# Paged attention on one core: moving the loads of the output weights to other slots of the first steps of each half

## Chip, cores and metric

The kernel runs on one core of a Trainium2 chip. The metric is the device time of the whole program in microseconds (us); lower is better.

## What is computed

```python
# x (64, 32, 512); 64 batches of 32 new tokens, 512 hidden, 32 query heads, 8 KV heads, D = 128
x = x + einsum('bct,bcd->bdt', x, W_cond[condition])      # a 32 x 32 matrix for each batch
q, k, v = x @ Wq.T, x @ Wk.T, x @ Wv.T                    # then RMS norm and RoPE on q and k
kc, vc = k_cache[block_table], v_cache[block_table]       # 16 pages of 32 rows: 512 cached keys a batch
scores = q @ concat(kc, k).T / sqrt(D)                    # cached keys masked by the sequence length
o = softmax(scores) @ concat(vc, v)                       # 4 query heads share a KV head
x = x + o.reshape(64, 32, 4096) @ Wo.T                    # output projection
```

All of it is in 32-bit floating point. The output weights Wo are 8 MB.

## The kernel before

**Halves, steps, slots.** The KV heads are taken in two halves (`NHH` = 2) of 4 heads (`GH`), with their 16 query heads each. The 64 batches are taken in 16 tiles (`NT`) of 4 batches (`BT`). A half and a tile make a step: step 0 to 15 are the first half, 16 to 31 the second (`st.n`; `st.t` is the tile, `st.hh` the half). The main loop (L901 to L976) goes through each step in 16 slots; a slot is one batch of the tile and one KV head, `slot = bt * GH + g`. Step 0 begins at slot 4, since its first batch is handled by an opening ahead of the loop.

**What a slot holds.** On TensorE (PE) each slot has the scores of a head (`ps`, L570) and the product with the values of the head before (`po`, L628): about 1.8 us. To this come pieces of the neighbouring steps. At slot 0 stand the scores of the new tokens (`psn`, L588), so that the first `psn` matmul marks the start of a step. At slot 3 stands the K projection of the step ahead (`pp_k`, L401), at slots 4 to 7 the four Q projections of the step ahead (`pp_q`, some 3.6 us each: the long slots), at slot 13 its V projection. At slots 8 and 9 stands the output projection of the step before (`out_proj`, L509 to L526, some 8 us in each of the two slots; slot 8 uses the weights of heads 0 and 1, slot 9 those of heads 2 and 3). At slot 14 the condition matrix is applied to the step after next (`pmix`, L357), and at slot 15 its result is transposed (`px1t`, L365) and copied; in the first half it is also written out for the second half (`x1_b`, L360 to L368: the DMA `x1t_d`, issued by ACT).

**Who orders the work.** The orders of SyncE (SP) and of PE are those in which the code issues (`manual_schedule`, L88); ACT, DVE and POOL are ordered by the scheduler. SP issues nearly all plain loads, in one queue, in this order within a step:

- `load_k` (L277 to L304), at slots 0, 4, 8 and 12, for the batch two ahead: 16 DMAs of 64 KB, one a page (`k_t`; two buffers, so that a load waits until DVE has copied the K of the batch two before it into `kh`, L563).
- `spread` (L460 to L468), at slot 9 (12 DMAs) and slot 11 (4 DMAs): the queries of the step ahead are rearranged, 80 KB each (`q_cols`, and `q_last` for the tile's last batch). The next step's `psn` needs all 16.
- `x1_t` (L341), at slot 13 of the second half: one DMA, read at slot 3 of the next step.
- the weight parts. `load_w` (L234 to L251) loads a quarter of a half's output weights as two parts; a part is 2 DMAs of 256 KB (`wo`, L249). 8 parts, 16 DMAs and 4 MB make up the output weights of a half.

POOL issues the gathers of V (`raw`, L315).

The programs as built show one more order. The DMAs that SP and ACT issue take their completion semaphores from one ring of eight, in turn. An instruction that issues a DMA first waits until the DMA eight places earlier in the ring has landed, whichever of the two engines issued it. Where a DMA of ACT stands in the ring is decided by the scheduler.

**The output weights before.** The rule at L955 asks for part `slot - 10 + st.t * 16` in the first two steps of each half: parts 0 to 5 at slots 10 to 15 of steps 0 and 16, parts 6 and 7 at slots 0 and 1 of steps 1 and 17. They are first read at slot 8 of steps 1 and 17.

Of the kernel before, what the change touches and what calls it, by code (L numbers as in the profile page):

```python
# [27 lines left out]
BT = P // S  # L28
NT = B // BT
NHH = 2  # L30
GH = HK // NHH
# [24 lines left out]
def cond_resid_paged_attention_kernel(  # L56
# [130 lines left out]
    def steps_of(exact, pools):  # L187
# [46 lines left out]
        def load_w(kind, hh, g=0, part=slice(0, 4), eng=nc.sync):  # L234
            if kind == "q":
                src = wq[:, (hh * QH + g * REP) * D : (hh * QH + (g + 1) * REP) * D]
            elif kind == "o":
                src = wo[(hh * QH + g * REP) * D : (hh * QH + (g + 1) * REP) * D, :]
            else:
                src = (wk if kind == "k" else wv)[:, hh * GH * D : (hh + 1) * GH * D]  # L240
            if part.start == 0:
                wt[kind, hh, g] = wpool.tile(
                    [P, 4, 512], F32, tag=f"w{kind}{g}", name=f"w{kind}{g}_{hh}_{uid}"
                )
            t = wt[kind, hh, g]
            if kind == "o" and not exact:
                src = src.rearrange("(h j p) e -> h p j e", h=REP, p=S)
                for h in range(part.start, part.stop):
                    nc.sync.dma_start(t[h * S : (h + 1) * S, :, :], src[h])  # L249
                return  # L250
            eng.dma_start(t[:, part, :], src.rearrange("(c p) e -> p c e", p=P)[:, part, :])  # L251

        def load_parts(which, hh, at):

            if 0 <= at < 2 * len(which):
                load_w(which[at // 2][0], hh, which[at // 2][1], slice(at % 2 * 2, at % 2 * 2 + 2))

        def load_cond_weights(t, eng=nc.sync, kind=mybir.EngineType.SP):
            _, number = nc.values_load_multi_w_load_instructions(
                cond_row[:, t, :],  # L260
                engines=[kind],
                min_val=0,
                max_val=NCOND - 1,
                skip_runtime_bounds_check_because="a batch's condition is one of those there are",
            )
            for i in range(BT):
                blk = slice(i * S, (i + 1) * S)
                eng.dma_start(
                    bd[blk, blk],
                    w_cond.rearrange("(n s) e -> n s e", s=S)[bass.ds(number[i], 1)].rearrange(  # L270
                        "o s e -> (o s) e"
                    ),
                )
# [67 lines left out]
        def x1_a(st):  # L341

            st.acc = work.tile([P, HID], F32, tag="acc", name=f"acc_{st.name}", bufs=3)
            src = acc_d[st.t] if st.hh else x[st.t * P : (st.t + 1) * P, :]
            nc.sync.dma_start(st.acc, src)
# [187 lines left out]
        def new_ot(st):  # L533
            st.ot = act.tile([P, QH, P], F32, tag="ot", name=f"ot_{st.name}", bufs=1)
# [31 lines left out]
        def scores(ba, g):  # L566

            ps = ps_s.tile([P, VC, P], F32, tag="ps", name=f"ps_{ba.name}_{g}")
            for c in range(VC):
                nc.tensor.matmul(  # L570
                    ps[:, c, :],
                    ba.k[g][:, c * P : (c + 1) * P],
                    queries(ba, g),
                    start=True,
                    stop=True,
                )
            pr = work.tile([P, VC, P], F32, tag="pr", name=f"pr_{ba.name}_{g}", bufs=3)
            last["act"] = nc.scalar.activation(pr, ps, AF.Exp, scale=SCALE).ins  # L578
            ba.pr[g] = pr
# [281 lines left out]
        def pieces(st):  # L861
            do = {
                2: (rot_tables,),
                3: (k_a,),
                4: ((q_a, 0),),
                5: ((q_a, 1),),
                6: ((q_a, 2),),
                7: ((q_a, 3),),
                9: ((spread, (0, 1, 3)),),
                11: ((spread, (2,)),),  # L870
                13: (v_a,),
            }
            if st is second:
                do[2] = do[3] = do[13] = ()
            return do
# [22 lines left out]

        x1_a(steps[2])
        load_cond_weights(2)  # L900
        for st in steps:  # L901
            ahead = steps[st.n + 1] if st.n + 1 < len(steps) else None
            beyond = steps[st.n + 2] if st.n + 2 < len(steps) else None
            fill = pieces(ahead) if ahead else {}
            for bt in range(0 if st.n else 1, BT):
                this, after = batch, None
                n = st.n * BT + bt + 2
                if n < NHH * NT * BT:
                    after = Batch(steps[n // BT], n % BT)
                    unfilled += [(after, c) for c in range(VC)]  # L910
                for g in range(GH):
                    slot = bt * GH + g
                    if st.n or slot > GH:
                        scores(this, g)
                    if slot == 0:
                        new_scores(st)
                    if slot in (1, 3):
                        new_values(st, slot - 1)
                    if slot < GH and valued is not None:
                        values(*valued)  # L920
                    for piece in fill.get(slot, ()):
                        if isinstance(piece, tuple):
                            piece[0](ahead, piece[1])
                        else:
                            piece(ahead)
                    if slot in (8, 9) and st.n:
                        out_proj(steps[st.n - 1], slice((slot - 8) * QH // 2, (slot - 7) * QH // 2))
                    if slot == 9:
                        if st.n:
                            new_ot(st)  # L930
                        for ba in turned:
                            turn(ba)
                        turned = []
                        if 0 < st.n < NT // TRIG - 1:
                            tmp = work.tile(
                                [P, 3, TRIG * HD], F32, tag="w1", name=f"trig_{st.n}", bufs=1
                            )
                            with tc.issue_after(last["dve"]), tc.issue_after(last["act"]):
                                angles((st.n + 1) * TRIG, tmp)
                    if slot == 10 and st.n:  # L940
                        store(steps[st.n - 1])
                    if st.n and beyond:
                        if slot == 6 and not beyond.hh:
                            load_cond_weights(beyond.t)
                        if slot == 11:
                            x1_a(beyond)
                    if slot == 13 and beyond:
                        x1_t(beyond)
                    if slot == 14 and beyond:
                        x1_c(beyond)  # L950
                    if slot == 15 and beyond:
                        x1_b(beyond)
                    if slot == 1 and st.n == NT:
                        count(0)
                    if st.t < 2:  # L955
                        load_parts([("o", i) for i in range(GH)], st.hh, slot - 10 + st.t * BT * GH)
                    if st.n in (NT - 2, NT - 1):
                        load_parts(
                            [("k", 0), ("q", 0), ("q", 1), ("q", 2), ("q", 3), ("v", 0)],
                            1,  # L960
                            slot - 5 + (st.n - NT + 2) * BT * GH,
                        )
                    for _ in range({1: 0, GH: 2}.get(slot, 1)):
                        if unfilled and (g or unfilled[0][0] is this):
                            next_values()
                    if slot >= GH and valued is not None:
                        values(*valued)
                    valued = this, g
                    if g == 1 and bt != 1:
                        for ba in turned:  # L970
                            turn(ba)
                        turned = []
                    if later is not None:
                        head_keys(later, g)
                turned.append(this)
                batch, later = later, after  # L976
# [75 lines left out]
```

## Time and profile before

| | us |
|---|---|
| median of three runs | 2204.2 (2204.06 to 2207.32) |
| profiled execution, whole time | 2204.06 |
| its span on the core | 2202.3 |
| first `psn` of steps 0, 1, 2, 3 | 58.27, 103.18, 193.77, 260.90 |
| a regular step of the first half (such as step 2) | 67.13 |
| step 1 | 90.59 |
| first `psn` of steps 16, 17, 18, 19 | 1131.38, 1197.30, 1275.02, 1340.94 |
| a regular step of the second half (such as step 18) | 65.9 |
| step 17 | 77.72 |

The span is the time from the core's first to its last instruction; 1.8 us lie around it. The lengths of the steps are the differences of the starts. A timeline row has the start, the busy time, the engine, the line of the program, the operation with its output and input, and the number of instructions; behind it, in brackets, the idle time before and what ended it. A row of waits has the waiting engine and line, what it waited for, and then the sum in us, the number of times and the longest.

### The profile page before, as it was taken

How to read it: one execution, taken by the hardware profiler on the slowest of the kernel's cores; microseconds unless marked ns; L12 is line 12 of the kernel's file. 1: busy time of each engine (PE TensorE's matmuls, PEld its weight loads, DVE VectorE, ACT ScalarE, POOL GpSimd, SP SyncE). 2: the span in 40 equal slices, each digit the busy share in tenths (PEclk: the TensorE clock that was granted, in tenths of full speed). 3: DMA queues.
4: the chain of work that ended last, by engine and by line, in shares of the span. 5: the costliest groups of instructions: out<-in, count | busy, mean ns of one | idle time of the engine just before them, and what ended most of it. 6: DMA issues, size and time to landing. Idle time of an engine off the chain costs nothing.

```text
span 2202.3 us, 41557 instructions
## 1 busy us (share of the span) xinstructions
PE 2156.6 (98%) x12970; PEld 1502.4 (68%) x12970; DVE 1198.1 (54%) x2881; ACT 867.5 (39%) x1574; POOL 806.1 (37%) x1008
## 2 busy tenths in 40 slices
PE   8889999999999999999999999999999999999998
PEld 5657766677766777666776567776667776667775
DVE  5545466655555654565554555445656445656442
ACT  3424444444333444333433244333334433334441
POOL 4423243333333433333333343334333334334330
PEclk9989999999999999999999999999999999999999
DMA  7575554555555555556766655655555655555551
GB/s 226 160 177 168 159 155 143 165 157 171 155 151 151 158 168 162 154 147 197 238 176 174 165 167 162 176 158 154 148 163 163 174 159 158 149 162 158 174 158 55
DMA packets 387863, 358.77 MB, mean 163 GB/s; under 512 B 54737, under 2 KB 316897, under 8 KB 387633
## 3 DMA queue, kind: packets, MB, share of 16 engines
q1 hardware_dynamic: 342912, 215.10, 34.9%
q0 software_dynamic: 41712, 136.66, 20.9%
q10 hardware_dynamic: 3008, 4.25, 0.5%
q8 instruction: 106, 1.74, 0.3%
q14 instruction: 125, 1.02, 0.2%
HBM read 302.59 MB, written 12.58 MB: 143 GB/s over the span
## 4 chain that ended last, share of the span: by engine, by line
PE 93%; DMA 3%; SPq 2%; issue 1%; ACT 1%; DVE 0%; POOL 0%; DVEq 0%; ACTq 0%; POOLq 0%
PE po_x L628 20%; PE pout_x L516 20%; PE ps_x L570 20%; PE pp_q_x L401 19%; PE pp_k_x L401 5%; PE pp_v_x L401 5%; PE pnv_x L612 2%; PE psn_x L588 1%; SPq L291 1%; DMA k_t_x<-in_kt_dram 1%; PE pmix_x L357 1%; DMA raw_x<-in_vc_dram,v_row 0%; DMA x1t_d<-x1t_x 0%; DMA x1t_x<-x1t_d 0%; DMA wq_x<-in_wq_dram 0%
## 5 line engine op out<-in xcount | busy, mean ns | idle before, releaser
L315 POOL DMA_INDIRECT raw_x<-in_vc_dram,v_row x512 | 538.8, 1052 | 837.9 <-ACT v_x L328 769.3
L578 ACT ACTIVATE pr_x<-ps_x 128x512 f32<-128x512 f32 x512 | 305.8, 597 | 837.4 <-PE ps_x L570 774.4
L628 PEld LDWEIGHTS po_x<-v_x,pr_x 128*128 128x128 f32 x4096 | 516.5, 192 | 125.5 <-issue 114.8
L628 PE MATMUL po_x<-v_x,pr_x 128*128 128x129 f32 x4096 | 551.8, 278 | 0.9 <-ACT v_x L328 0.6
L401 PE MATMUL pp_q_x<-wq_x,x1t_x 128*128 128x512 f32 x1024 | 465.0, 597 | 2.8 <-DMA wq_x<-in_wq_dram 2.8
L516 PE MATMUL pout_x<-wo_x,ot_x 128*128 128x512 f32 x1024 | 451.6, 594 | 0.0
L570 PE MATMUL ps_x<-q_cols_x,kh_x 128*128 128x128 f32 x3072 | 408.7, 276 | 14.2 <-DVE kh_x L563 13.7
L570 PEld LDWEIGHTS ps_x<-q_cols_x,kh_x 128*128 128x128 f32 x3072 | 378.7, 193 | 31.9 <-issue 26.4
L328 ACT ACTIVATE v_x<-raw_x,valid 128x512 f32<-128x512 f32 x512 | 363.0, 716 | 11.6 <-DMA raw_x<-in_vc_dram,v_row 11.2
L516 PEld LDWEIGHTS pout_x<-wo_x,ot_x 128*128 128x128 f32 x1024 | 190.5, 191 | 215.1 <-issue 214.9
L401 PEld LDWEIGHTS pp_q_x<-wq_x,x1t_x 128*128 128x128 f32 x1024 | 186.5, 192 | 189.6 <-issue 186.4
L563 DVE COPY kh_x<-k_t_x 128x512 f32<-128x512 f32 x506 | 205.2, 417 | 181.4 <-PE ps_x L570 151.2
L646 DVE TENSOR_TENSOR nv_x<-po_x,nv_x 128x258 f32<-128x258 f32 x256 | 108.4, 423 | 341.3 <-PE po_x L628 319.9
L418 POOL TENSOR_TENSOR rs_q_x<-ms_q_x,minus_half 128x4 f32<-128x4 f32 x128 | 140.4, 1097 | 176.3 <-DVE ms_q_x L416 176.3
L411 ACT ACTIVATE sq_q_x<-pp_q_x 128x512 f32<-128x512 f32 x128 | 76.6, 598 | 273.6 <-PE pp_q_x L401 186.7
L570 PE MATMUL ps_x<-q_last_x,kh_x 128*128 128x128 f32 x1024 | 135.3, 275 | 0.0
L524 DVE TENSOR_TENSOR acc_x<-pout_x,acc_x 128x512 f32<-128x512 f32 x32 | 22.1, 692 | 200.2 <-PE pout_x L516 200.2
L570 PEld LDWEIGHTS ps_x<-q_last_x,kh_x 128*128 128x128 f32 x1024 | 124.6, 192 | 0.0
L401 PE MATMUL pp_k_x<-wk_x,x1t_x 128*128 128x512 f32 x256 | 117.7, 603 | 3.1 <-DMA x1t_x<-x1t_d 3.0
L415 DVE TENSOR_REDUCE ms_q_x<-sq_q_x 128x4 f32<-128x512 f32 x128 | 86.5, 676 | 54.4 <-ACT sq_q_x L411 52.7
L401 PE MATMUL pp_v_x<-wv_x,x1t_x 128*128 128x512 f32 x256 | 115.2, 592 | 0.0
L649 DVE TENSOR_TENSOR o_x<-nv_x,rden 128x256 f32<-128x256 f32 x256 | 108.5, 424 | 6.5
(105 smaller groups left out, 1464.6 us busy)
## 6 DMA issues: line engine op xcount, KB each, us to landing
k_t_x<-in_kt_dram SPq DMA_DIRECT2D x2048, 64.0 KB
q_cols_x<-rows_x SPq DMA_DIRECT2D x372, 80.0 KB
q_last_x<-rows_x SPq DMA_DIRECT2D x124, 80.0 KB
raw_x<-in_vc_dram,v_row POOLq DMA_INDIRECT x512
wo_x<-in_wo_dram SPq DMA_DIRECT2D x32, 256.0 KB
acc_x<-in_x_dram SPq DMA_DIRECT2D x16, 256.0 KB
x1t_d<-x1t_x ACTq DMA_DIRECT2D x16, 256.0 KB
acc_d<-acc_x SPq DMA_DIRECT2D x16, 256.0 KB
```

The lines of the kernel that those rows point to most:

```text
L315: nc.gpsimd.indirect_dma_start(out=raw.rearrange("p g d -> p (g d)"), out_offset=None, in_=vc, in_offset=bass.IndirectOffsetOnAxis(ap=v_ro ...
L328: nc.scalar.activation(v_bufs[b % 2][:, c, :, 0:D], raw, AF.Copy, scale=ok)
L401: nc.tensor.matmul(pp, st.x1t[:, c, :], w[:, c, :], start=(c == 0), stop=(c == KC - 1))
L415: nc.vector.tensor_reduce(ms, sq, AX.X, ALU.add)
L418: nc.gpsimd.tensor_tensor(rs, ms, minus_half, ALU.pow)
L516: nc.tensor.matmul(st.po, st.ot[:, i, :], wt["o", st.hh, i // 4][:, i % 4, :], start=(i == 0), stop=(i == QH - 1),)
L563: last["dve"] = nc.vector.tensor_copy(k, ba.k_raw[:, :, g, :]).ins
L570: nc.tensor.matmul(ps[:, c, :], ba.k[g][:, c * P : (c + 1) * P], queries(ba, g), start=True, stop=True,)
L578: last["act"] = nc.scalar.activation(pr, ps, AF.Exp, scale=SCALE).ins
L628: nc.tensor.matmul(ba.po[:, g % 2, :], ba.pr[g][:, c, :], ba.v_t[:, c, g, :], start=(c == 0), stop=(c == VC - 1),)
L646: nc.vector.tensor_tensor(t, ba.po, t, ALU.add)
L649: nc.vector.tensor_tensor(ba.o[:, both, :], t[:, :, 0:D], rd.unsqueeze(2).to_broadcast([P, 2, D]), ALU.mult,)
```

## The change

The rule for the output weights is replaced by a table from step and slot to parts.

```diff
+        output_weights = {
+            (0, 4): (0, 1),
+            (0, 5): (2, 3),
+            (0, 6): (4, 5),
+            (1, 4): (6,),
+            (1, 5): (7,),
+            (NT, 10): (0,),
+            (NT + 1, 2): (1,),
+            (NT + 1, 4): (2,),
+            (NT + 1, 5): (3, 4),
+            (NT + 1, 6): (5, 6),
+            (NT + 1, 7): (7,),
+        }
...
-                    if st.t < 2:
-                        load_parts([("o", i) for i in range(GH)], st.hh, slot - 10 + st.t * BT * GH)
+                    for at in output_weights.get((st.n, slot), ()):
+                        load_parts([("o", i) for i in range(GH)], st.hh, at)
```

In the first half parts 0 to 5 (12 DMAs, 3 MB) move from slots 10 to 15 of step 0 to its slots 4 to 6, and parts 6 and 7 from slots 0 and 1 of step 1 to its slots 4 and 5. In the second half part 0 stays at slot 10 of step 16; parts 1 to 5 move from slots 11 to 15 of step 16, and parts 6 and 7 from slots 0 and 1 of step 17, to slots 2 to 7 of step 17. Within a slot the parts stand where they stood: behind the K load, the pieces and `x1_b`.

In the built program the change also moves instructions of engines that the scheduler orders. The place of step 0's last `x1t_d` in the ring of eight goes from between the third and fourth `q_last` DMA of the spread to between the ninth and tenth `wo` DMA. On DVE, the copies `kh` of batch 5 go from behind the norm and rotation of step 1's K to ahead of them, and those of batch 6 and of batch 70 (the third batch of steps 1 and 17) from behind the rotation of the fourth Q projection to between the projections, as they stand in every other step.

## The prediction

> **What bounds the kernel now.** The page's first part says which engine carries the time, its table of waits which waits that engine has.
>
> ```profile
> PE 2156.6 (98%) x12970; PEld 1502.4 (68%) x12970; DVE 1198.1 (54%) x2881; ACT 867.5 (39%) x1574; POOL 806.1 (37%) x1008
> ```
> ```profile
> PE ps_x L570 <- DVE kh_x L563: 13.7, 4, 4.8
> PE psn_x L588 <- DMA q_cols_x<-rows_x: 8.8, 1, 8.8
> ...
> PE pp_k_x L401 <- DMA x1t_x<-x1t_d: 3.0, 1, 3.0
> ```
>
> PE is the bound, and what a load can still give is PE's waits. Where they lie is read from the starts of the steps: all are regular but two. Step 1 takes 90.59 us against 67.13 (23.46 too many), step 17 takes 77.72 against 65.9 (11.8 too many). So the change can gain at most about 35 us, in two places, and I read those two alone. First PE's timeline:
>
> ```profile
> 112.49 0.39 PE L588 MATMUL psn_x<-q_cols_x 128*32 128x128 f32 x1 [8.77 <-DMA q_cols_x<-rows_x]
> ...
> 130.54 1.61 PE L570 MATMUL ps_x<-q_cols_x,kh_x 128*128 128x128 f32 x8 [3.07 <-DVE kh_x L563]
> ...
> 158.20 1.88 PE L570 MATMUL ps_x<-q_cols_x,kh_x 128*128 128x128 f32 x8 [4.83 <-DVE kh_x L563]
> ```
> ```profile
> 1210.08 5.17 PE L401 MATMUL pp_k_x<-wk_x,x1t_x 128*128 128x512 f32 x8 [3.01 <-DMA x1t_x<-x1t_d]
> ...
> 1240.97 2.04 PE L570 MATMUL ps_x<-q_cols_x,kh_x 128*128 128x128 f32 x8 [4.84 <-DVE kh_x L563]
> ```
>
> Step 1 waits 8.77 + 3.07 + 4.83 = 16.7 us; the other 6.8 are matmuls at a low clock after each wait (the scores take 1.6 to 2.0 us there, 1.06 in a regular step). Step 17 waits 7.85 us, and some 4 go the same way. What fed them late stands in SP's timeline:
>
> ```profile
> 93.09 4.85 SPq L465 DMA_DIRECT2D q_cols_x<-rows_x  x8
> 97.99 4.07 SPq L465 DMA_DIRECT2D q_last_x<-rows_x  x4
> 102.10 1.07 SPq L249 DMA_DIRECT2D wo_x<-in_wo_dram  x2
> 103.27 3.07 SPq L465 DMA_DIRECT2D q_cols_x<-rows_x  x4
> 110.61 0.88 SPq L249 DMA_DIRECT2D wo_x<-in_wo_dram  x2
> 112.78 8.75 SPq L291 DMA_DIRECT2D k_t_x<-in_kt_dram  x16
> ```
> ```profile
> 1203.27 3.84 SPq L249 DMA_DIRECT2D wo_x<-in_wo_dram  x6
> 1208.41 15.75 SPq L291 DMA_DIRECT2D k_t_x<-in_kt_dram  x16
> ```
>
> In step 0 the last 4 DMAs of the spread are issued by 106.34 and land 6 us later. SP then stands from 106.34 to 110.61. Its table of waits names the reason, and this is the ring of eight at work: the second part's DMA has to wait for ACT's `x1t_d`, issued at 103.56.
>
> ```profile
> SPq L249 <- DMA x1t_d<-x1t_x: 4.2, 1, 4.2
> ```
>
> How busy the transfers are, the table by windows shows (busy times, then granted clock, DMA share, GB/s):
>
> ```profile
> 60.00:90.00 30.00, 29.05 (x180) 20.84 (x180) 20.47 (x51) 13.85 (x28) 13.38 (x16) 1.00 0.40 116
> 90.00:120.00 30.00, 20.61 (x183) 18.90 (x181) 9.80 (x27) 11.56 (x21) 9.43 (x12) 0.83 0.82 210
> ```
>
> The weights are asked for in the full stretch, just after one that is 0.40 full.
>
> **Second half.** Out of step 16's end go 10 `wo` DMAs (parts 1 to 5), out of slots 0 and 1 of step 17 another 4. On SP the `x1t` load stood behind 4 of them and was issued at 1202.81, followed at once by 6 more, and landed some 7 us later. Without them the K load for batch 69, from 1189 or 1190, takes 8.2 us instead of 11.32; `x1t` goes at about 1198 and lands near 1200, or at 1205 if it took 7 us again; it is needed at 1207. The wait of 3.01 goes. The 4.84 is one of DVE's order: before, the four copies for batch 70 stand behind the rotation of the fourth projection; in the built program of after they stand between the projections, as in every regular step. What is late next could be the weights. The K load for batch 71 stands ahead of 12 of the 14; it waits for its buffer, the copies of batch 69, and runs from about 1208 to 1216. Then the 12 are issued by 1222 to 1226 (0.48 each at best). Of 210 GB/s the gathers of V keep 62 (136.66 MB in the page's software queue, over the span), which leaves 3 MB some 20 us: parts 2 and 3 are in by 1223 to 1226, the last by 1233 to 1237. Slot 8 comes at about 1232 and reads parts 0 to 3, slot 9 at 1241 the rest. I take no wait. Step 17 becomes regular: 11.8 less 0.3 for small waits = **11.5 us**; the low end is 8, with one wait of 3 us left.
>
> **First half, what goes.** 12 `wo` DMAs move to slots 4 to 6 of step 0, where SP stands idle from 73.8 to 84.6: 12 x 0.48 = 5.8 us of issue fit in. The stretch moves 116 GB/s where 210 to 217 are shown, so 94 GB/s are free and 3 MB need at most 33 us; the kernel's start moved 280 GB/s, which makes it 19. The copies for batches 5 and 6 move on DVE as in step 17, so the waits of 3.07 and 4.83 go.
>
> **First half, what comes.** `x1t_d` now stands in the ring between the ninth and tenth `wo` DMA. Eight places on comes the fifth of 16 DMAs of the K load for batch 4. SP stands there until `x1t_d` has landed, which is made at slot 15. Behind it on SP wait 12 DMAs of that K load, all 16 of the spread, then the K load for batch 5; PE's next step waits for all the spread. No trace shows this wait; its nearest row is SP's own stand of 4.2 us above. Working: `x1t_d` is issued at 102.3 to 103.5 (before: 103.56, of which 1.31 were ACT's wait for a V gather). Its landing has two rows: 7.0 us in the full stretch (103.56 to 110.6), and 2.05 for the one at 49.62. SP stands still ahead of it here and the weights are in by some 95, so I take 2.05: 104.4 to 105.6, middle 105. [...] So the 7.0 stays the other end here: 5 us more. From 105: 12 x 0.515 = 6.2, 16 x 0.62 = 9.9, ends at 121; 2 us to land: `psn` at **122.9** (bounds 121.5 and 128), against 112.49.
>
> From there step 1 is regular but for the cold start. One start after 8.77 us took about 2.4 us (8 `po` took 2.09 for 1.06). A wait of 20 us could cost more; [...] I take the row. So step 1 ends at 122.9 + 67.1 + 2.4 = 192.4, where before it ended at 193.77: **1.4 us** gained, from 2.8 down to -3.7. The cover: the K load for batch 5 runs on SP from 121 to 129.5 and lands at 132 (needed about 138), that for batch 6 lands at about 142 (needed about 155), parts 6 and 7 at 155 (needed 167). If it slips by more than 6 us, PE waits again for `kh`.
>
> Later steps: the place of `x1t_d` in the ring is the same in all of them. Nothing is counted.
>
> **Sum.** 11.5 + 1.4 = 12.9; against the profiled execution 2204.06 - 12.9 = 2191.2; the median is 2204.2, 0.1 above: about **2191.5**. With both ends, 2189.5 to 2200.
>
> **Rivals.** (a) The stand does not cost, because `x1t_d` comes sooner or the wait is short. Then the spread follows the K load as before, `psn` comes at about 106: 6.5 us, and with 3.07 + 4.83 + 3.6 of low clock step 1 gains 18; 2204 - 29.5 = 2174.5. For it speaks the empty stretch; against it, that `x1t_d` is made at slot 15 by the order of PE. 0.08. (b) The weights of step 17 come late, since they share the transfers with two K loads (0.97 of the engines were busy from 1200 to 1220): `out_proj` waits 4 to 7 us in slots 8 and 9 and restarts cold: 2196 to 2199. 0.13. (c) The change doesn't make up for its new stand: both effects near cancel, step 17 wins half and step 1 loses 3 to 6: 2200 to 2208. 0.07. (d) Slower: the stand is long. Place: the fifth DMA of the K load for batch 4. Price: a microsecond of `psn` for each one that `x1t_d` lands later. It evens out at 122.9 + 1.4 + 11.5 = 136, so when `x1t_d` lands after 118, and is slower by 0.2% from 122.5 on. ACT would have to stand 15 us ahead of it, behind a gather of V that the weights' 3 MB hold up; at 20 us: 2211. The page gives ACT's waits for gathers 11.2 us over the whole run, 1.31 the one here. 0.07. The likeliest case, as worked out, has 0.65, with its own range 2188 to 2197.
>
> **Numbers.** A measurement of this kernel can tell 0.2%, 4.4 us, from no change. Faster holds the likeliest case, (a) and most of (b): 0.84. Same: (c) and the rest: 0.09. Slower: (d): 0.07. The range 2184 to 2200 holds the likeliest case and (b), with the better half of step 1's cover; (a), (c) and (d) are left out.
>
> **What would show it.** Right: in SP's timeline 4 DMAs of the K load for batch 4, a stand until about 105 put down to `x1t_d`, 12 more, then the spread; PE's one long wait at `psn` (18 to 20 us) ending near 123; no wait for `kh` in steps 1 and 17; step 17 at about 66.2. Wrong: `psn` before 115 or after 130, waits for `kh` at slots 4 and 8 as before, or `out_proj` waiting for `wo`.

## The result, and the profile after

| | before | after |
|---|---|---|
| median of five runs, us | 2204.32 (2204.06 to 2207.32) | 2192.11 (2190.95 to 2196.1) |
| ratio | | 0.9952, 95% interval 0.994 to 0.9964 |
| profiled execution | 2204.06 | 2190.95 |
| steps 0 and 1 together (first `psn` of step 0 to first `psn` of step 2) | 135.50 | 136.34 |
| step 17 | 77.72 | 65.89 |
| from the first `psn` of step 31 to the end | 70.69 | 69.06 |

The kernel became 12.2 us faster; 2191.5 had been predicted. The gain that can be told lies in step 17 (11.8 us). Steps 0 and 1 together became 0.8 us longer in the profiled execution, which is less than kernels with the same first half differ by (see below the table of runs). (From here on they are taken together, since in the changed kernel PE's long wait lies partly ahead of the first `psn` and so counts to step 0.) The 1.6 us at the end are not the change's: this stretch took 68.8 to 72.5 us in the runs below, with no relation to what they change.

**The second half.** In SP's timeline of the changed kernel `x1t`, a single DMA, now follows the K load at once, with no weights around it:

```profile
1189.75 9.07 SPq L291 DMA_DIRECT2D k_t_x<-in_kt_dram  x16
1198.84 0.33 SPq L351 DMA_DIRECT2D x1t_x<-x1t_d  x1
1200.60 9.19 SPq L291 DMA_DIRECT2D k_t_x<-in_kt_dram  x16
1209.84 0.91 SPq L249 DMA_DIRECT2D wo_x<-in_wo_dram  x2
1212.03 8.26 SPq L291 DMA_DIRECT2D k_t_x<-in_kt_dram  x16
1220.33 9.40 SPq L249 DMA_DIRECT2D wo_x<-in_wo_dram  x12
```

`x1t` is asked for 4.0 us sooner (1202.81 before), the K load for batch 70 starts 7.8 us sooner and takes 9.19 instead of 15.75. In step 17 PE has no wait left, neither for `x1t` nor for `kh`, and none for the weights, although the last of these are issued only at 1229.7. PE reads the first weights at 1232.03.

**The first half.** PE's table of waits and its timeline show two waits where there were three, and they are longer:

```profile
PE ps_x L570 <- DMA q_cols_x<-rows_x: 12.6, 1, 12.6
PE psn_x L588 <- DMA q_cols_x<-rows_x: 5.3, 1, 5.3
```
```profile
116.85 2.05 PE L570 MATMUL ps_x<-q_cols_x,kh_x 128*128 128x128 f32 x8 [12.62 <-DMA q_cols_x<-rows_x]
...
125.25 0.61 PE L588 MATMUL psn_x<-q_cols_x 128*32 128x128 f32 x2 [5.33 <-DMA q_cols_x<-rows_x]
```

Together 17.95 us, against 16.7 before. The two waits for `kh` are gone. What PE waits for is the spread, and SP's timeline and its waits from 72 to 125 us say why it is late:

```profile
73.54 11.02 SPq L249 DMA_DIRECT2D wo_x<-in_wo_dram  x12
86.98 25.53 SPq L291 DMA_DIRECT2D k_t_x<-in_kt_dram  x16
112.69 5.06 SPq L465 DMA_DIRECT2D q_cols_x<-rows_x  x8
117.80 2.49 SPq L465 DMA_DIRECT2D q_last_x<-rows_x  x4
120.38 2.43 SPq L465 DMA_DIRECT2D q_cols_x<-rows_x  x4
```
```profile
SPq L291 <- DMA x1t_d<-x1t_x: 14.7, 1, 14.7
SPq L249 <- DMA wo_x<-in_wo_dram: 5.2, 4, 2.5
SPq L291 <- DMA wo_x<-in_wo_dram: 3.9, 4, 1.5
```

The K load for batch 4 stretches over 25.5 us instead of 8.1, and 14.7 of them are one stand (SP issues nothing): four DMAs are issued, and the fifth waits until 106.5 for the `x1t_d` that ACT issues at 104.10. The traces of both kernels show the ring by the semaphores themselves: the 2752 DMAs of SP and ACT raise eight of them, 344 times each, and 2695 of SP's 2728 wait, before they are issued, for the one that they raise. `x1t_d` raises the fifth K DMA's: the last raise is at 106.50, that DMA is issued at 106.51. In the kernel before the pair was `x1t_d` and the `wo` DMA behind the spread, at 110.59 and 110.61. The windows show that around the stand the transfers have room: the share from 60 to 90 rose from 0.40 to 0.77, that from 90 to 120 fell from 0.82 to 0.61, and from 92 to 106 alone it is 0.62.

```profile
60.00:90.00 30.00, 29.05 (x165) 20.28 (x165) 19.57 (x47) 12.68 (x25) 12.25 (x14) 0.94 0.77 182
90.00:120.00 30.00, 16.21 (x122) 14.45 (x121) 9.51 (x26) 10.00 (x17) 9.25 (x12) 0.82 0.61 161
```

### The profile page after: what moved, and what is told of

Same layout as the page of the kernel before. It is cut to its first block, busy times and chain, and to the rows that moved or that the text cites. A ratio compares the mean times of both kernels' runs of the same rounds, so it can differ in the third digit from the quotient of the medians.

```text
span 2189.2 us, 41546 instructions
## 1 busy us (share of the span) xinstructions
PE 2151.3 (98%) x12970; PEld 1500.0 (69%) x12970; DVE 1199.7 (55%) x2881; ACT 867.3 (40%) x1574; POOL 806.1 (37%) x1008
## 3 DMA queue, kind: packets, MB, share of 16 engines
q10 hardware_dynamic: 3008, 4.25, 0.5%
## 4 chain that ended last, share of the span: by engine, by line
PE 97%; DMA 1%; SPq 1%; issue 0%; ACT 0%; DVE 0%; ACTq 0%; DVEq 0%
PE po_x L628 22%; PE ps_x L570 21%; PE pout_x L516 20%; PE pp_q_x L401 20%; PE pp_v_x L401 5%; PE pp_k_x L401 5%; PE pnv_x L612 2%; PE psn_x L588 2%; PE pmix_x L357 1%; SPq L465 0%; DMA wq_x<-in_wq_dram 0%; SPq L291 0%; PE px1t_x L365 0%; DMA x1t_d<-x1t_x 0%; DMA w_sel<-in_w_cond_dram,cond 0%
## 5 line engine op out<-in xcount | busy, mean ns | idle before, releaser
L524 DVE TENSOR_TENSOR acc_x<-pout_x,acc_x 128x512 f32<-128x512 f32 x32 | 22.1, 692 | 199.5 <-PE pout_x L516 199.5
```

## The experiments

The theory: step 17 gives the whole gain, some of it because `x1t` comes sooner and the larger part because DVE's order goes with the loads; in the first half the stand behind `x1t_d`, which comes from the ring and not from the weights, eats what the freed stretch gives. The main rivals: both halves gain, and step 17's wait was for the K load and not for DVE's order.

All runs at a glance. Each median stands beside one of the kernel before, measured next to it on the same chip; the lengths of steps are from the profiled execution of each, in us.

| run | median | before | ratio (95%) | steps 0 + 1 | step 17 |
|---|---|---|---|---|---|
| the change | 2192.11 | 2204.32 | 0.9952 (0.994 to 0.9964) | 136.34 | 65.89 |
| first_half_only | 2205.47 | 2203.33 | 1.001 (1.0001 to 1.002) | 137.84 | 78.27 |
| second_half_only | 2192.15 | 2203.33 | 0.9947 (0.9933 to 0.9961) | 134.80 | 65.94 |
| x1t_by_sync | 2180.45 | 2203.33 | 0.9891 (0.9875 to 0.9908) | 122.83 | 65.92 |
| old_slots_x1t_by_sync | 2191.91 | 2203.33 | 0.9955 (0.994 to 0.9971) | 134.81 | 65.96 |
| late_weights_x1t_by_sync | 2186.71 | 2202.9 | 0.9923 (0.9907 to 0.9939) | 128.49 | 65.90 |
| late_weights | 2189.19 | 2202.9 | 0.9938 (0.9924 to 0.9952) | 129.50 | 65.94 |
| parts_1_to_5_moved | 2193.17 | 2202.9 | 0.9957 (0.9941 to 0.9972) | 136.14 | 65.95 |
| late_copies | 2196.67 | 2202.9 | 0.997 (0.9958 to 0.9981) | 135.48 | 70.93 |
| four_parts_ahead | 2173.61 | 2200.35 | 0.9874 (0.9859 to 0.9889) | 118.63 | 65.83 |
| two_parts_ahead | 2177.3 | 2200.35 | 0.9886 (0.9869 to 0.9903) | 122.78 | 65.83 |
| parts_6_7_moved | 2201.02 | 2200.35 | 1.0001 (0.9991 to 1.0011) | 134.19 | 77.65 |
| four_parts_by_act | 2192.4 | 2201.27 | 0.9961 (0.9947 to 0.9975) | 135.70 | 65.93 |

Five of these kernels have the same first half: the change, first_half_only, parts_1_to_5_moved, late_copies and parts_6_7_moved. Their steps 0 and 1 take 134.19 to 137.84 us. So a difference of up to some 3.6 us in that column, seen in one profile of each, tells nothing by itself. Step 17 has no such scatter: in the nine kernels with the change's second half it takes 65.83 to 65.96.

### One half at a time

`first_half_only` keeps the new slots of steps 0 and 1 and writes the old slots of the second half into the table (the cut below); `second_half_only` is the reverse.

```diff
             (NT, 10): (0,),
-            (NT + 1, 2): (1,),
...
+            (NT, 11): (1,),
...
+            (NT + 1, 1): (7,),
```

> The change in the first half alone; the second half keeps its old slots. Theory (the new stand on SP eats what the freed stretch gives): step 1 ends about 0.7 us later than before, as in the changed kernel, step 17 stays at 77.7: 2203.5 to 2206. Rival (the first half has its share in the gain, as the forecast had it): 2203 or less; if it carried half of the 12 us, 2198.

> The change in the second half alone; the first half keeps its old slots. Theory: step 17 is regular (65.9 instead of 77.7), step 1 takes 90.6 as before: 2204.3 - 11.8 = 2192.5, the same as the whole change within a microsecond. Rival (both halves needed): 2194 to 2199.

The first half alone gives 1.001 with an interval just above 1: nothing gained, 2 us lost if anything. The second half alone gives what the whole change gives. The theory holds on both. The 1.4 us that were forecast for the first half would be a ratio of 0.9994; this run excludes it. parts_6_7_moved below has the same first half and a step 17 as long as before, and gives 1.0001 (0.9991 to 1.0011). Together: no gain to be seen, and a loss of some 2 us if any.

### The stand in the ring

`x1t_by_sync` is the whole change with one DMA issued by another engine. SP issues it later than ACT did (at 122.49 instead of 104.10), since it stands behind slot 12's K load; nothing in the first half reads it.

```diff
-            nc.scalar.dma_start(x1t_d[st.t], st.x1t.rearrange("p c q -> p (c q)"))
+            eng = nc.sync if st.n == 2 else nc.scalar
+            eng.dma_start(x1t_d[st.t], st.x1t.rearrange("p c q -> p (c q)"))
```

> The whole change, but the one x1t_d of step 0's slot 15 is issued by SP, behind the K load of slot 12, instead of by ACT, so that it stands at SP's own place in the ring and no K load waits for it. Theory (the ring held SP for 14.7 us): no stand; the K load for batch 4 is issued from 87 to 95.5, the spread from 95.5 to 105.5, psn at about 107.5 instead of 125.25, step 1 ends about 18 us sooner: 2174. Rival (the spread is late for another reason, the queries or the transfers' rate): psn after 115, 2182 or more.

2180.45: most of the gain is there, but the `psn` of 107.5 is not. SP's timeline and its waits in the same stretch, and PE's timeline:

```profile
86.10 14.19 SPq L291 DMA_DIRECT2D k_t_x<-in_kt_dram  x16
100.41 5.82 SPq L466 DMA_DIRECT2D q_cols_x<-rows_x  x8
```
```profile
SPq L291 <- DMA wo_x<-in_wo_dram: 4.7, 5, 1.5
SPq L249 <- DMA wo_x<-in_wo_dram: 3.8, 4, 1.6
```
```profile
108.02 1.98 PE L571 MATMUL ps_x<-q_cols_x,kh_x 128*128 128x128 f32 x8 [3.44 <-DMA q_cols_x<-rows_x]
...
113.48 0.41 PE L589 MATMUL psn_x<-q_cols_x 128*32 128x128 f32 x2 [2.31 <-DMA q_cols_x<-rows_x]
```

The stand behind `x1t_d` is gone, and PE waits for the spread 5.75 us instead of 17.95. The K load still takes 14.2 us: the first of its DMAs now wait for `wo` DMAs eight places ahead (4.7 us in five waits), with 3 MB under way and the 16 DMA engines 0.94 to 1.07 busy from 70 to 110. So theory and rival both have a share: the stand cost 13.5 us of steps 0 and 1 (136.34 to 122.83; against the other kernels with the same first half 11.4 to 15.0), and the number of parts asked for ahead looks like a second cost that the stand had hidden. four_parts_ahead below tests it.

`old_slots_x1t_by_sync` puts the same edit on the old slots of the first half.

> Second half new, first half with its old slots, and the x1t_d of step 0's slot 15 issued by SP. Theory (in the old order the stand on the ring was only 4.2 us, and the rest of step 1's loss comes from weights in the full stretch and from DVE's order): psn stays near 112, the wait for kh of 3.07 shrinks, that of 4.83 stays: 2188 to 2192.5. Rival (the ring alone made step 1 long, whatever the slots): as x1t_by_sync, 2174 to 2178.

Against `second_half_only` it changes nothing that can be told (2191.91 and 2192.15): SP's stand of 4.2 us was not what made step 1 long before the change. PE's waits for `kh` stay at 3.07 and 4.83 (the first had been expected to shrink), and DVE's order is the old one: its timeline has the copies for batch 6 behind the fourth rotation, at 156.21.

### How many parts ahead of the spread

The next two runs leave one part in step 0, at slot 10, and put the other seven into step 1: the second half's slots in the first half too, `x1t_d` by SP in one and by ACT in the other.

```diff
-            (0, 4): (0, 1),
-            (0, 5): (2, 3),
-            (0, 6): (4, 5),
-            (1, 4): (6,),
-            (1, 5): (7,),
+            (0, 10): (0,),
+            (1, 2): (1,),
+            (1, 4): (2,),
+            (1, 5): (3, 4),
+            (1, 6): (5, 6),
+            (1, 7): (7,),
```

> The second half as changed; the first half gets the second half's slots (part 0 at slot 10 of step 0, parts 1 to 7 at slots 2 to 7 of step 1), and x1t_d of step 0's slot 15 is issued by SP. Theory (of the first half's loss two causes are left: the ring and 3 MB that go ahead of the spread): the K load for batch 4 runs from 85 to 93, the spread ends at about 104, psn at about 106, step 1 at about 67 to 70 us and no wait for kh: 2172 to 2175. Rival (the weights come late now and out_proj of step 1 waits): 2180 or more.

> The same slots, x1t_d left to ACT. In the built program its place in the ring falls between the third and fourth q_last DMA, as before the change, so that the next in its place is the first DMA of the K load for batch 5, behind the whole spread. Theory (a stand costs by what is queued behind it): psn as in late_weights_x1t_by_sync, the K load for batch 5 starts when x1t_d has landed, at about 106, in time: 2172 to 2176. Rival (any stand behind x1t_d costs its length): 4 us or more above the other.

Both miss: 2186.71 and 2189.19, slower than `x1t_by_sync`. Neither the theory's size nor the rival's reason was right; `out_proj` waited for nothing. Two things are late, in PE's timeline of late_weights_x1t_by_sync:

```profile
107.49 0.39 PE L589 MATMUL psn_x<-q_cols_x 128*32 128x128 f32 x1 [6.99 <-DMA q_cols_x<-rows_x]
176.69 1.99 PE L357 MATMUL pmix_x<-acc_x,bd 128*128 128x512 f32 x2 [4.25 <-DMA acc_x<-in_x_dram]
```

The second is new. The `acc` load (slot 11; the input of `pmix`) stands on SP behind the K load of slot 8 and the spread, and these in step 1 now stand behind 12 late `wo` DMAs; `acc` is issued at 173.95 (166.10 in four_parts_ahead below, where PE does not wait for it). The second half has no `pmix`, and so the same slots cost nothing there. On the ring the two differ as expected: with ACT's `x1t_d` there is a stand of 3.5 us behind the spread, ahead of the K load for batch 5. Steps 0 and 1 together take 129.50 against 128.49, within the scatter, and the intervals of the two ratios overlap: this stand costs nothing that can be told.

`four_parts_ahead` and `two_parts_ahead` go between the two ends, with `x1t_d` by SP. The edit of the first, against the change:

```diff
-            (0, 6): (4, 5),
-            (1, 4): (6,),
-            (1, 5): (7,),
+            (1, 4): (4, 5),
+            (1, 5): (6, 7),
```

> As x1t_by_sync (the whole change, x1t_d of step 0's slot 15 issued by SP), but only parts 0 to 3 are asked for in slots 4 and 5 of step 0; parts 4 to 7 in slots 4 and 5 of step 1. Theory (a DMA ahead of the spread delays psn by its transfer, one in step 1 delays acc for pmix): 1 MB less ahead of the K load gives psn some 3 to 4 us sooner than 113.5, pmix not late: 2176 to 2178. Rival (the spread is bound by the gathers of V and not by the weights): 2180 to 2182, as x1t_by_sync.

> As four_parts_ahead with two parts in slot 4 of step 0 and six in slots 2 to 6 of step 1. Theory: psn at 107 to 109, the acc load of step 1 late by 1 to 4 us at pmix: 2177 to 2184. Rival (the fewer ahead the better): 2174 to 2176.

Four parts ahead has the lowest ratio of all, 0.9874 against 0.9952 for the change: 26.7 us under the kernel before. (Its interval overlaps that of two parts ahead, 0.9886.) Its SP and PE timelines:

```profile
72.34 5.28 SPq L249 DMA_DIRECT2D wo_x<-in_wo_dram  x8
84.19 8.17 SPq L291 DMA_DIRECT2D k_t_x<-in_kt_dram  x16
92.55 5.10 SPq L466 DMA_DIRECT2D q_cols_x<-rows_x  x8
97.69 2.49 SPq L466 DMA_DIRECT2D q_last_x<-rows_x  x4
100.27 3.15 SPq L466 DMA_DIRECT2D q_cols_x<-rows_x  x4
```
```profile
106.74 0.38 PE L589 MATMUL psn_x<-q_cols_x 128*32 128x128 f32 x2 [2.57 <-DMA q_cols_x<-rows_x]
```

Eight `wo` DMAs are issued by 77.6, the K load begins at 84.19 and runs without a stand in 8.17 us; `psn` has 2.57 us of wait left and `pmix` none. So fewer parts ahead of the K load do let it run (8.17 us instead of 14.19). With two parts ahead `psn` is as good (2.88 us), and the late weights cost at `pmix`:

```profile
175.46 1.12 PE L357 MATMUL pmix_x<-acc_x,bd 128*128 128x512 f32 x2 [3.42 <-DMA acc_x<-in_x_dram]
```

The theory's direction held, its size was too small (2176 to 2178 for four parts, 2173.61 measured).

`four_parts_by_act` is the same with `x1t_d` left to ACT, as in the kernel before.

> four_parts_ahead with x1t_d left to ACT; in the built program its place in the ring is the one behind the eighth wo DMA, so that the eighth of the 16 DMAs of the K load for batch 4 waits for it. Theory (the stand sets psn, whatever the weights): x1t_d in at about 106, then 9 K DMAs and the spread, 4.6 + 9.9 + 2.4: psn at about 123 instead of 106.7, some 16 us over four_parts_ahead and 1 to 3 under the whole change: 2188 to 2191, a ratio of about 0.994 to the kernel before. Rival (moving weights was what made four_parts_ahead fast): 2174 to 2178, a ratio under 0.989.

SP's timeline, its waits and PE's timeline of this run:

```profile
85.16 24.60 SPq L291 DMA_DIRECT2D k_t_x<-in_kt_dram  x16
```
```profile
SPq L291 <- DMA x1t_d<-x1t_x: 15.0, 1, 15.0
```
```profile
122.81 0.61 PE L588 MATMUL psn_x<-q_cols_x 128*32 128x128 f32 x2 [5.58 <-DMA q_cols_x<-rows_x]
```

A stand of 15.0 us, `psn` at 122.81 (about 123 expected), and steps 0 and 1 at 135.70, as in the kernel before and in the change. The median is 1.4 us above the theory's range, and far from the rival's. The issuing engine of this one DMA is worth 17.1 us of steps 0 and 1 here (135.70 less 118.63). With SP issuing it, four parts ahead are worth 16.2 us against the old slots (134.81 less 118.63); with ACT, nothing (134.80 in second_half_only, 135.70 here).

### What made step 17 long

`parts_1_to_5_moved` leaves parts 6 and 7 at slots 0 and 1 of step 17 and moves 1 to 5; `parts_6_7_moved` does the reverse.

```diff
             (NT, 10): (0,),
-            (NT + 1, 2): (1,),
-            (NT + 1, 4): (2,),
+            (NT + 1, 0): (6,),
+            (NT + 1, 1): (7,),
+            (NT + 1, 4): (1, 2),
             (NT + 1, 5): (3, 4),
-            (NT + 1, 6): (5, 6),
-            (NT + 1, 7): (7,),
+            (NT + 1, 6): (5,),
```

> First half as changed. Second half: parts 6 and 7 at their old slots 0 and 1 of step 17, parts 1 to 5 moved to slots 4 to 6 of step 17. Theory (what held up x1t and the K load for batch 70 were the parts asked for at the end of step 16): step 17 at 66 to 67, 2192 to 2193. Rival (parts 6 and 7, ahead of the K load for batch 71 on SP, hold it up): step 17 at 70 or more, 2196.

> First half as changed. Second half: parts 0 to 5 at their old slots 10 to 15 of step 16, parts 6 and 7 moved to slots 6 and 7 of step 17. Theory: x1t and the K load for batch 70 stand behind the weights as before, and DVE's order is the old one: waits of some 3 and 4.8 us, step 17 at 76 to 78, 2203. Rival (4 DMAs fewer ahead of the K load for batch 71 are enough): step 17 under 70, 2196.

Step 17 takes 65.95 in the first and 77.65 in the second. So the 10 DMAs at the end of step 16 made the step long, and the 4 ahead of the K load for batch 71 did nothing. PE's timeline of parts_6_7_moved has both of the old waits:

```profile
1207.81 5.24 PE L401 MATMUL pp_k_x<-wk_x,x1t_x 128*128 128x512 f32 x8 [3.52 <-DMA x1t_x<-x1t_d]
...
1238.77 2.05 PE L570 MATMUL ps_x<-q_cols_x,kh_x 128*128 128x128 f32 x8 [4.84 <-DVE kh_x L563]
```

`late_copies` keeps the change's transfers and puts DVE's four copies of batch 70's K back behind the fourth projection's rotation (its sum, L435).

```diff
+            last["turn"] = nc.vector.tensor_tensor(r, r, u, ALU.add).ins
...
-                    if later is not None:
+                    if later is not None and later.n == (NT + 1) * BT + 2:
+                        if g == GH - 1:
+                            with tc.issue_after(last["turn"]):
+                                for h in range(GH):
+                                    head_keys(later, h)
+                    elif later is not None:
                         head_keys(later, g)
```

> The whole change with its transfers; on DVE the four copies of batch 70's K are put behind the rotation of step 17's fourth Q projection, where they stood before the change. Theory (the wait of 4.84 was DVE's order and not the K load): PE waits about 4.8 us for kh at slot 8 of step 17 and loses about 1.8 at a low clock: step 17 at 72.5, 2198.7. Rival (the K load was late and the order did not matter): step 17 at 66, 2192.

The wait comes back with the transfers of the change (the K load is issued by 1207.97), so the order makes it. It is 3.04 instead of 4.84 us: the first copy stands right behind the sum, and before the change it stood behind the rotation's last product and the transpose too. PE's timeline of late_copies, and below it the same place in the changed kernel:

```profile
1232.03 1.13 PE L570 MATMUL ps_x<-q_cols_x,kh_x 128*128 128x128 f32 x8 [3.04 <-DVE kh_x L563]
1233.00 8.73 PE L516 MATMUL pout_x<-wo_x,ot_x 128*128 128x512 f32 x16
```
```profile
1232.03 7.03 PE L516 MATMUL pout_x<-wo_x,ot_x 128*128 128x512 f32 x16
```

Step 17 is 5.04 us longer than in the change (70.93 less 65.89): 3.04 of wait, and 1.70 in the 16 matmuls behind it. Of the 11.8 us of step 17 before, the order on DVE is some 6.3: 4.84 of wait, and 1.5 in the scores and the 16 matmuls behind it (2.04 and 7.54 us, where the change has 1.05 and 7.03). The late `x1t` is some 4.5: 3.01 of wait, and 1.5 in the K projection behind it. PE's timelines of the kernel before, and below it of the changed kernel:

```profile
1242.81 7.54 PE L516 MATMUL pout_x<-wo_x,ot_x 128*128 128x512 f32 x16
```
```profile
1206.76 3.66 PE L401 MATMUL pp_k_x<-wk_x,x1t_x 128*128 128x512 f32 x8
```

About 1 us is left over. Both parts follow from the same 10 DMAs: with these at the end of step 16 the built program has the copies behind the fourth rotation (parts_6_7_moved), with these moved it has them between the projections (parts_1_to_5_moved). That the scheduler puts the copies late because the K load comes late is a likely reason and not shown.

## Why the prediction was right, point by point

- **Step 17, 11.5 us.** Measured 11.83. The wait for `x1t` and that for DVE's copies went and none came in `out_proj`, as worked out; late_copies shows the part of DVE's order, parts_1_to_5_moved and parts_6_7_moved which loads bring both waits. `x1t` was issued at 1198.84 (about 1198 forecast). The 12 DMAs were issued until 1229.7 instead of 1226: SP waited some 4 us of it for DMAs eight places ahead (9.40 us instead of 5.8), without cost.
- **The stand on `x1t_d`.** As forecast in place and size: four K DMAs, a stand put down to `x1t_d`, 12 more, the spread. PE's wait came in two pieces, 12.62 and 5.33, where one of 18 to 20 had been named as the sign. It ended at 125.25. The prediction's own terms add up to 123.1 and not to the 122.9 that it gives (105 + 6.2 + 9.9 + 2). The 2.15 us from there are small terms: `x1t_d` was issued at 104.10 instead of about 102.9 (1.2), landed in 2.4 us instead of 2.05 (0.35), the spread took 10.1 instead of 9.9 (0.2), and landed in 2.4 instead of 2 (0.4). The first is within the scatter: in the five kernels with this first half `x1t_d` was issued between 100.57 and 104.10. In all five SP stood for it (14.6 to 16.7 us) and the wait ended 20.7 to 22.1 us after its issue, against 20.2 forecast; this is the better test of the mechanism. The choice between a landing of 2.05 us (the quiet row) and 7.0 (the loaded one) fell right: the transfers had room. Of three such DMAs, 256 KB each, those of 2.05 and 2.4 us were under way at a DMA share of 0.34 and 0.54, the one of 7.0 at 0.96.
- **The cold start, 2.4 us.** From 125.25 to the next step's first `psn` it took 69.25 us; a regular step has 66.6 from that point (67.13 less the 0.55 of the four `psn` ahead of the wait). That is 2.65 (2.0 to 3.5 in the five kernels with this first half). (The prediction counted a whole step and 2.4 from there, 69.5 us, so that 0.25 too much stood in this term.) It is not a test of a longer gap. The granted clock was 0.50 from the start of work at 116.85 until 129.57, and what ran slowly between the two waits cost nothing, since a wait followed; the 2.65 stand behind a gap of 5.33. The windows show for how long PE worked at 0.50 behind a wait: 4.93 us behind 8.77 in the kernel before (112.49 to 117.42; some 2.4 lost), 4.32 behind the 5.33 here (125.25 to 129.57; 2.65 lost), and in step 17 before 3.02 behind 3.01 (from 1210.08; 1.5 lost) and 2.85 behind 4.84 (from 1240.97; 1.5 lost); in late_copies 1.70 were lost behind 3.04. In the four measured both ways the losses go roughly with that time, at 0.49 to 0.61 of it, and not with the wait's own length. The row at `psn` was the right one to take for this place; what sets how long the clock stays low was not shown.
- **The first half, 1.4 us gained.** This gain did not come: 0.8 us lost in the profiled execution, 1.001 (1.0001 to 1.002) in first_half_only, 1.0001 (0.9991 to 1.0011) in parts_6_7_moved. It was a difference of two large numbers, with bounds from 2.8 down to -3.7, and smaller than the scatter of the very steps it speaks of; its sign could hardly be forecast. The mechanism that it counts, DVE's waits gone and a stand in their place, is what the traces show. That the total came out 0.6 us from the median is partly luck: in the profiled execution 1.6 us at the end, which the change does not touch, stand where the first half's gain is missing.
- **Rival (a), no stand: 2174.5.** It did not happen, but it names what the change gives away. With the stand taken out, x1t_by_sync came to 2180.45 only: the spread does not follow the K load as before, since with 3 MB ahead the K load itself takes 14.19 us instead of 8.17. With 2 MB ahead, four_parts_ahead came to 2173.61. The prediction has this cost at nothing (12 DMAs in 5.8 us of issue); in the changed kernel they took 11.02 us, and the K load's first DMAs waited 3.9 us for them, which the stand behind covered.
- **Rivals (b), (c) and (d).** No wait for weights in `out_proj`, and ACT's waits for a gather of V in the 15 us ahead of `x1t_d` were 1.23, 2.02 and 0.21 us, so (b) and (d) had no part. (c) is wrong on the second half, which kept its whole gain; the 3 to 6 us that it has the first half lose are not seen either.

What stays open: why `psn` waits 7 us in late_weights_x1t_by_sync, with hardly any weights ahead, and 2.6 in four_parts_ahead. A likely reason is part 0, whose 0.5 MB stands between the first 12 DMAs of the spread and its last 4. SP's timeline of late_weights_x1t_by_sync:

```profile
94.76 2.94 SPq L466 DMA_DIRECT2D q_last_x<-rows_x  x4
97.74 1.09 SPq L249 DMA_DIRECT2D wo_x<-in_wo_dram  x2
98.94 2.44 SPq L466 DMA_DIRECT2D q_cols_x<-rows_x  x4
```

From the end of the last issue, 101.38, to the end of PE's wait it is 6.1 us. The records speak for this reason: in all five kernels that have `wo` DMAs at this place (the kernel before, second_half_only, old_slots_x1t_by_sync and the two with late weights) this stretch is 6.1 to 7.1 us, in the nine others 1.9 to 3.9. It was not tried by itself: the transfers were full too, 0.96 from 90 to 107.

## What to carry to other kernels

A load that is moved moves everything behind it on its queue, and where two engines take completion semaphores from one ring, as SP and ACT do in this program, it can move the place of the other engine's DMA too: look up which instruction is eight places on, and what is queued behind that (here a stand of 14.7 us, ahead of 12 K DMAs and the spread). When a large block of loads goes into a free stretch, ask how much fits before the next urgent load begins; here 8 DMAs fitted (a K load of 8.17 us), 12 delayed the spread (14.19), and with 4 or 2 the rest pushed a later load (3.42 and 4.25 us of wait at `pmix`). A wait on a copy can be the copying engine's order, which the scheduler chose, and not the load's lateness (3.04 us in late_copies); moving loads can change that order too, as here. And before a gain of 1 us is forecast in some steps, see by how much these steps differ between kernels that are alike there.

## What was not expected of the hardware

An `x1t_d` of 256 KB landed in 7.0 us in the full stretch (DMA share 0.96) and in 2.4 us once SP stood still (0.54). Behind a wait of PE of 3.04 us the granted clock was already lower (0.86 from 1226 to 1236 in late_copies, 1.00 in the change; 16 matmuls took 8.73 us instead of 7.03). Two waits of 12.62 and 5.33 us with 3 us of slow work between them cost 2.65 behind the second, hardly more than the 2.4 behind one of 8.77. The kernel before itself had medians from 2200.35 to 2204.32 us in the five groups of runs, so that only ratios to the one measured beside it are compared here.
